# Gram chain of a four-layer convolution kernel: outer products from diagonals and one constant product, copies merged, one link fewer

## The chip, the cores and the metric

The kernel runs on one core of a Trainium2 chip. The metric is device time in microseconds (us), the median of the runs. TensorE is called PE, VectorE DVE, ScalarE ACT, GpSimd POOL; SP is SyncE, which issues most of the DMAs.

## The reference

The input x is 16 images of 64 channels by 128 by 128 pixels, float32. Each of four layers adds to x something computed from a group norm of x (32 groups, so two channels in each).

```python
def _L0_conv_ref(x, conv_w):
    N = H * W
    xf = x.reshape(B, C, N)
    gram = jnp.einsum('bcn,bdn->bcd', xf, xf) / N
    y = jnp.einsum('bcd,bdn->bcn', gram, xf)
    y = y.reshape(B, C, H, W)
    out = jnp.einsum('oc,bchw->bohw', conv_w, y)
    return out
...
x = x + _L0_conv_ref(_gn(x), L0_conv_conv_w)
x = x + _L1_conv_ref(_gn(x))                         # |gx| + |gy| of a 3x3 edge filter in each channel
x = x + _L2_conv_ref(_gn(x), L2_conv_W, L2_conv_b)   # shift of half of the channels by a column, 3x3 conv
x = x + _L3_conv_ref(_gn(x), L3_conv_w_bin, ...)     # 3x3 conv, 1x1 conv, norm over the batch, leaky, clip
```

Layer 0 is linear in the pixels once the Gram matrix of the image (64 by 64) is known. With the channel means mu and the group means and variances, the layer is one 64 by 64 matrix A for each image, and so are the group statistics of its output.

## The kernel before

**Layout.** An image's 64 channels stand twice on the 128 partitions, upper and lower half of the picture, and it is worked in NS = 8 pieces of R = 8 rows of each half. Most matrix products are of 64 columns of weights, and are issued to the two column halves of PE by turns (`small_product` does that for the small ones: two products of 128x64 weights).

**Order of the work.** The order on each engine is written out by hand and kept. A main loop runs over steps; a step is one piece of each of three stages that work on different images at the same time, Layer3, Layer2 and Front (layers 0 and 1: `mix` multiplies by A into the tile `po`, ACT writes the normalized tile `xh`, DVE makes the edge filter from it in `u` and `e`). Each step has quarters 0 to 3. In each quarter the stages issue their share: in quarter 1 the four DVE operations of the edge filter, ahead of quarter 2 the two Abs of ACT on `u` and `e`, in quarter 2 and 3 the DVE operations that read these.

**Gram matrices.** For each image the class Gram reads x with pixels on the partitions (`xr`), ACT copies it to `xw`, and 128 products add up the Gram matrix and the sums in `pg`. Then `gram_chain` is appended to a list of generators, `chains`. At the end of each quarter `tick()` advances each chain to its next `yield`, so every link of a chain is issued behind that quarter's other work. Most links are one PE product or the DVE operations between two products. A link is a quarter of a step after the one before it. The lines `if b > 1: yield` split links for images 2 to 15; image 1 has the shorter chain of nine ticks, and image 0's chain runs by itself, before the loop, in `first_gram`, where ACT copies pieces of image 1's `xr` between links 2 to 6. Images 1 to 6 are prepared at double pace.

**The chain itself.** `gs`: copy of `pg`. `gd`: sum of both halves. `g`: Gram matrix and means `mu`. `st0`: means and the Gram matrix's diagonal. A product with `gavg` takes the average over each group. `rstd` makes 1/sqrt(variance + eps) from that: `me`, `nv`, `var`, Sqrt on ACT into `sd`, then a reciprocal and a refinement to `r`. `vv` holds five columns of means. Four small vectors turned to rows by `pr` and copied to `rw` give an outer product of two rows each, `pc`, so that `cs` is the covariance of the centred channels, twice side by side. `pq` multiplies by the layer's weights `rc`; `ad`, `wbd` and `abd` are A in the shapes needed; `pd`, `pp`, `av` and `pk` give mean and second moment of the layer's output, from which a second `rstd` makes the coefficients `co1` for Front. `coefficients` is the like chain for the norms ahead of layers 2 and 3.

All tiles of the small products lie in one bank of PSUM, and are called `bank` in the profile. All instructions issued through the ordered engines have the line of the helper, L73; they are told apart by the names of their tiles.

Of the kernel before, what the change touches and what calls it, by code (L numbers as in the profile page):

```python
# [10 lines left out]
F32 = mybir.dt.float32  # L11
AF = mybir.ActivationFunctionType
ALU = mybir.AluOpType
AX = mybir.AxisListType

B, C, H, W = 16, 64, 128, 128
P = 128
# [5 lines left out]
EARLY = 3  # L23
CP = 4
GN_EPS = 1e-5
# [19 lines left out]
def single(table, n):  # L45

    for o in range(2):
        planes = [i for m, i, half, _ in table if (m, half) == (n, o)]
        if len(planes) == 1:
# [1 line left out]

NAMES = [("I", P), ("same", P), ("hsame", P), ("gavg", P), ("gmean", P), ("bnavg", P), ("Id", C), ("q", 1),
         ("keep0", 1), ("keep1", 1), ("left", 1), ("right", 1), ("I3", 3 * P), ("lower", 1), ("upper", 1)]
AT = {}
K_END = 0
# [20 lines left out]
def constants():  # L78
    k = np.zeros((P, K_END), np.float32)
    p = np.arange(P)  # L80
    ch = p % C

    def put(name, a):
        k[:, AT[name][0]:AT[name][1]] = a

    same = ch[:, None] == ch[None, :]
    pair = ch[:, None] // 2 == ch[None, :] // 2
    put("I", np.eye(P))
    put("same", same)
    put("hsame", 0.5 * same)  # L90
    put("gavg", 0.25 * pair)
    put("gmean", pair / (2.0 * HW))
    put("bnavg", (ch[:, None] == (p // 2)[None, :]) / (B * HW))
    put("Id", ch[:, None] == np.arange(C)[None, :])
    put("q", 0.25)
    put("keep0", (~((ch >= C // 4) & (ch < C // 2)))[:, None])
    put("keep1", (~(ch < C // 4))[:, None])

    left, right = ch < C // 4, (ch >= C // 4) & (ch < C // 2)
    put("left", left[:, None])  # L100
    put("right", right[:, None])
    put("I3", np.concatenate([np.eye(P) * m[:, None] for m in (left, ~left & ~right, right)], axis=1))
    put("lower", (p < C)[:, None])
    put("upper", (p >= C)[:, None])
    return k
# [3 lines left out]
def tile_kernel(ctx: ExitStack, tc: tile.TileContext, x, cw_h, w2_t, b2, wbin_t, w1_t, b1, gamma, beta, consts, out):  # L109
# [10 lines left out]
    def k(name):  # L120
        return kc[:, AT[name][0]:AT[name][1]]
# [41 lines left out]
    def sv(name, n=1):  # L163
        return small.tile([P, n], F32, tag=name, name=name)
# [16 lines left out]
    def sm(n, rows=P):  # L181
        if n > 8:
            return bank[0:rows, P:P + n]
        turn[0] = (turn[0] + 1) % 16
        return bank[0:rows, 8 * turn[0]:8 * turn[0] + n]
# [72 lines left out]
            if next(c, chains) is chains:  # L258
                chains.remove(c)

    def rstd(mE, eps):

        me = sv("me", 2)
        dve.tensor_copy(me, mE)
        nv = sv("nv")
        dve.scalar_tensor_tensor(nv, me[:, 0:1], me[:, 0:1], me[:, 1:2], op0=ALU.mult, op1=ALU.subtract)
        var = sv("var")
        dve.tensor_scalar(var, nv, -1.0, eps, op0=ALU.mult, op1=ALU.add)
        sd = sv("sd")
        act.activation(sd, var, AF.Sqrt)  # L270
        yield
        r0 = sv("r0")
        dve.reciprocal(r0, sd)

        e = sv("e")
        dve.scalar_tensor_tensor(e, var, r0, r0, op0=ALU.mult, op1=ALU.mult)
        dve.tensor_scalar(e, e, -0.5, 1.5, op0=ALU.mult, op1=ALU.add)
        r = sv("r")
        dve.tensor_mul(r, r0, e)
        return r, me[:, 0:1]  # L280

    def coefficients(st, put, back=None):

        s2 = sv("s2", 2)
        dve.tensor_reduce(s2, st, axis=AX.X, op=ALU.add)
        yield
        pm = sm(2)
        small_product(pm, k("gmean"), s2)
        yield
        r, mean = yield from rstd(pm, GN_EPS)  # L290
        co = sv("co", 2) if back is None else sv("co2", 6)
        dve.tensor_copy(co[:, 0:1], r)
        dve.scalar_tensor_tensor(co[:, 1:2], mean, -1.0, r, op0=ALU.mult, op1=ALU.mult)
        if back is not None:

            dve.reciprocal(co[:, 2:3], r)
            dve.tensor_mul(co[:, 3:4], co[:, 2:3], k("left"))
            dve.tensor_mul(co[:, 4:5], co[:, 2:3], k("right"))
            dve.tensor_add(co[:, 5:6], mean, back)
        put(co)  # L300
# [4 lines left out]
    def gram_chain(b, pg):  # L305

        gs = stp.tile([P, C + 1], F32, tag="gs", name=f"gs_{b}", bufs=1)
        dve.tensor_copy(gs, pg)
        if b > 1:
            yield  # L310
        gd = sm(C + 1)
        small_product(gd, k("same"), gs)
        yield
        g = stp.tile([P, C + 1], F32, tag="g", name=f"g_{b}", bufs=1)
        dve.tensor_scalar_mul(g, gd, 1.0 / HW)
        mu = g[:, C:C + 1]
        st = sv("st0", 2)
        dve.tensor_copy(st[:, 0:1], mu)
        junk0 = stp.tile([P, C], F32, tag="junk0", name=f"junk0_{b}", bufs=1)
        dve.scalar_tensor_tensor(  # L320
            junk0, g[:, 0:C], 1.0, k("Id"), op0=ALU.mult, op1=ALU.mult, accum_out=st[:, 1:2]
        )
        if b > 1:
            yield
        pm = sm(2)
        small_product(pm, k("gavg"), st)
        yield
        r, mean = yield from rstd(pm, GN_EPS)

        vv = sv("vv", 5)  # L330
        dve.tensor_scalar_mul(vv[:, 0:1], mu, -1.0)
        dve.tensor_sub(vv[:, 1:2], mu, mean)
        dve.tensor_copy(vv[:, 2:3], mu)
        dve.tensor_sub(vv[:, 3:4], mu, mean)
        dve.tensor_scalar_mul(vv[:, 4:5], mean, -1.0)
        if b > 1:
            yield
        pr = sm(2 * P, rows=2)
        pe.matmul(pr[:, 0:P], vv[:, 0:2], k("hsame"), start=True, stop=True)
        pe.matmul(pr[:, P:2 * P], vv[:, 2:4], k("hsame"), start=True, stop=True)  # L340
        yield
        rw = stp.tile([2, 2 * P], F32, tag="rw", name=f"rw_{b}", bufs=1)
        dve.tensor_copy(rw, pr)
        if b > 1:
            yield
        pc = sm(C)
        pe.matmul(pc, rw[:, 0:P], rw[:, P:P + C], start=True, stop=True)
        yield

        cs = stp.tile([P, 2, C], F32, tag="cs", name=f"cs_{b}", bufs=1)  # L350
        for s in range(2):
            dve.tensor_add(cs[:, s, :], pc, g[:, 0:C])
        rc = stp.tile([P, C], F32, tag="rc", name=f"rc_{b}", bufs=1)
        dve.tensor_scalar(rc, cwh, r, 0.5, op0=ALU.mult, op1=ALU.mult)
        csf = cs.rearrange("p s c -> p (s c)")
        if b > 1:
            yield
        pq = sm(C)
        small_product(pq, csf, rc)
        yield  # L360
        r2 = sv("r2")
        dve.tensor_mul(r2, r, r)
        for s in range(2):
            rows = slice(s * C, (s + 1) * C)
            dve.tensor_scalar_mul(wbd[rows, rows], pq[rows], r2[rows])
        ad = stp.tile([P, C], F32, tag="ad", name=f"ad_{b}", bufs=1)
        dve.scalar_tensor_tensor(ad, pq, r2, k("Id"), op0=ALU.mult, op1=ALU.add)
        abd = stp.tile([P, P], F32, tag="abd", name=f"abd_{b}", bufs=EARLY + 3)
        dve.tensor_add(abd, wbd, k("I"))
        if b > 1:  # L370
            yield
        pd = sm(C + 3)
        small_product(pd[:, 0:C], csf, ad)
        small_product(pd[:, C:C + 2], abd, vv[:, 2:4])
        small_product(pd[:, C + 2:C + 3], wbd, vv[:, 4:5])
        yield
        pp = stp.tile([P, 2, C], F32, tag="pp", name=f"pp_{b}", bufs=1)
        for s in range(2):
            dve.tensor_mul(pp[:, s, :], pd[:, 0:C], ad)
        av = sv("av", 3)  # L380
        dve.tensor_copy(av, pd[:, C:C + 3])
        if b > 1:
            yield
        pk = sm(1)
        small_product(pk, pp.rearrange("p s c -> p (s c)"), k("q"))
        if b > 1:
            yield
        bias = sv("bias")
        dve.tensor_copy(bias, av[:, 2:3])
        st1 = sv("st1", 2)  # L390
        dve.tensor_add(st1[:, 0:1], av[:, 0:1], bias)
        t = sv("t1")
        dve.scalar_tensor_tensor(t, av[:, 1:2], av[:, 1:2], pk, op0=ALU.mult, op1=ALU.subtract)
        dve.scalar_tensor_tensor(
            st1[:, 1:2], st1[:, 0:1], st1[:, 0:1], t, op0=ALU.mult, op1=ALU.subtract
        )
        if b > 1:
            yield
        pm = sm(2)
        small_product(pm, k("gavg"), st1)  # L400
        yield
        r, mean = yield from rstd(pm, GN_EPS)

        co = stp.tile([P, 4], F32, tag="co1", name=f"co1_{b}", bufs=EARLY + 3)
        dve.tensor_copy(co[:, 0:1], r)
        dve.tensor_sub(co[:, 1:2], bias, mean)
        dve.tensor_mul(co[:, 1:2], co[:, 1:2], r)
        dve.reciprocal(co[:, 2:3], r)
        dve.tensor_copy(co[:, 3:4], mean)
        lead[b] = abd, co  # L410

    def gram_product(pg, w):
# [696 lines left out]
```

## Time and profile before

| | |
|---|---|
| median of 3 runs | 2795.21 us (2790.94 to 2795.56) |
| profiled execution | 2793.34 us, span of the instructions 2791.6 us |
| granted PE clock, mean | 0.900 |
| PE busy | 2232.5 us (80%), 14836 matmuls |
| DVE busy | 2200.6 us (79%), 3751 instructions |
| ACT busy | 2115.3 us (76%), 3177 instructions |
| POOL busy | 865.2 us (31%), 1350 instructions |
| DMA | 685.97 MB, mean 246 GB/s |

Busy time is the union of an engine's intervals. A float32 matmul appears as two records. In a line of the profile the tile written stands left of the arrow, those read right of it; `bank<-kc,vv` is a product that writes the small bank from a constant and `vv`. A line of waits says which engine and tile waited for whom, total us, times, longest us. A timeline line has start and duration in us, and in brackets how long the engine had been idle and what ended it. The duration of neighbouring DVE operations overlaps, so that the start-to-start distance says what an operation costs.

The span has four stages: the start to 47 us with image 0's Gram matrix and chain bare; 47 to 350 us, in which Layer2 and Layer3 come in and the Gram matrices of images 1 to 6 are made; 350 to 2325 us with all stages; and an end of 470 us in which layer 3's norm over the batch is applied and everything is read and written once more.

### The profile page before, as it was taken

Reading aid. Unit: us, or ns where it says so; the run is one execution under the profiler, and the core shown is the slowest. Engines: PE = TensorE matmul, PEld = TensorE weight load, DVE = VectorE, ACT = ScalarE, POOL = GpSimd, SP = SyncE. Lnnn points to the kernel's source line nnn. Section 1 sums busy time; section 2 is a strip of 40 time slices with the busy share of each in tenths; the row PEclk is TensorE's granted clock in tenths of the full one; section 3 lists DMA queues with packets and bytes.
Section 4 is the critical chain, followed back from the end, with each engine's and each line's share of the span. In section 5 each row is a group of like instructions: output and inputs, shape, how many; then the busy total and the mean of one; then the engine's idle time right before and its main releaser. Section 6 shows DMA issues by size and latency. Waiting matters only on the chain. (4 is left out here: it accounts for less than half of the span.)

```text
span 2791.6 us, 46444 instructions
## 1 busy us (share of the span) xinstructions
PE 2232.5 (80%) x14836; PEld 1097.1 (39%) x14836; DVE 2200.6 (79%) x3751; ACT 2115.3 (76%) x3177; POOL 865.2 (31%) x1350
## 2 busy tenths in 40 slices
PE   6578899999999999999999999999999995000000
PEld 4234444534454444353534343466666641000000
DVE  4998999898989898989898989999996435333332
ACT  4666789888888888888888888998997667333332
POOL 2054434342434343334343434444444310000000
PEclk8689999999999999999999999999999997555555
DMA  7789878888888888888888867888887768999999
GB/s 193 196 224 235 223 203 237 218 228 211 222 222 219 222 221 224 221 220 220 223 219 225 215 182 198 213 205 216 208 208 185 214 194 277 419 420 420 420 420 390
DMA packets 680290, 685.97 MB, mean 246 GB/s; under 512 B 60096, under 2 KB 580448, under 8 KB 680048
## 3 DMA queue, kind: packets, MB, share of 16 engines
q1 hardware_dynamic: 654896, 613.83, 74.4%
q0 software_dynamic: 25152, 69.18, 10.1%
q8 instruction: 120, 1.97, 0.3%
q14 instruction: 122, 1.00, 0.1%
HBM read 346.23 MB, written 268.44 MB: 220 GB/s over the span
## 5 line engine op out<-in xcount | busy, mean ns | idle before, releaser
L73 PE MATMUL two<-d,w 128*64 128x508 f32 (+2 forms) x2560 | 898.7, 587 | 0.0
L73 PE MATMUL two<-d,wi 128*64 128x508 f32 (+3 forms) x1536 | 629.8, 576 | 0.0
L73 POOL DMA_DIRECT2D qd<-d x512 | 270.8, 531 | 892.5 <-issue 330.2
L73 PE MATMUL two<-qd,pk 128*64 128x512 f32 (+1 forms) x1024 | 518.6, 588 | 3.1 <-DMA qd<-d 2.4
L73 POOL TENSOR_SCALAR edges<-v,co 64x8 f32<-64x8 f32 x512 | 330.0, 645 | 355.6 <-ACT v L73 240.4
L73 PE MATMUL po<-x,abd 128*64 128x512 f32 x1024 | 385.9, 626 | 50.3 <-ACT xh L73 47.7
L73 PEld LDWEIGHTS two<-d,w 128*64 128x64 f32 x2560 | 297.4, 136 | 289.5 <-issue 219.5
L73 PE MATMUL one<-v,w 128*64 128x508 f32 (+2 forms) x1600 | 409.6, 578 | 0.0
L73 PE MATMUL one<-v,wi 128*64 128x508 f32 (+3 forms) x1536 | 408.9, 590 | 0.0
L73 DVE TENSOR_TENSOR d<-v 128x512 f32<-128x512 f32 (+1 forms) x512 | 346.0, 679 | 41.5 <-POOL v L73 16.7
L73 ACT COPY qd<-d 64x512 f32<-64x512 f32 x512 | 315.4, 616 | 21.0 <-DVE d L73 14.6
L73 ACT ACTIVATE xh<-po,co 128x128 f32<-128x128 f32 (+1 forms) x480 | 274.9, 621 | 62.4 <-PE po L73 58.9
L73 DVE SCALAR_TENSOR_TENSOR e<-e 128x1032 f32<-128x1032 f32 (+1 forms) x256 | 313.4, 1224 | 0.0
L73 DVE SCALAR_TENSOR_TENSOR y<-two,c 128x1024 f32<-128x1024 f32 x128 | 156.1, 1220 | 129.8 <-ACT v L73 71.5
L73 PEld LDWEIGHTS two<-d,wi 128*64 128x64 f32 x1536 | 196.3, 135 | 146.4 <-issue 110.7
L73 POOL TENSOR_SCALAR v<-v,kc 128x9 f32<-128x9 f32 x256 | 234.8, 930 | 11.9
L73 ACT ACTIVATE v<-x,co 128x512 f32<-128x512 f32 (+2 forms) x368 | 234.9, 705 | 0.0
L73 PEld LDWEIGHTS one<-v,w 128*64 128x64 f32 x1600 | 163.4, 137 | 178.3 <-issue 128.6
L73 PEld LDWEIGHTS one<-v,wi 128*64 128x64 f32 x1536 | 156.2, 138 | 163.0 <-issue 126.1
L73 ACT ACTIVATE u<-u 128x1024 f32<-128x1024 f32 x128 | 135.3, 1057 | 88.4 <-DVE u L73 87.0
L73 DVE SCALAR_TENSOR_TENSOR u<-xh 128x1170 f32<-128x1170 f32 x128 | 175.7, 1373 | 6.0 <-ACT xh L73 4.4
L73 PEld LDWEIGHTS two<-qd,pk 128*64 128x64 f32 x1024 | 128.6, 136 | 120.3 <-issue 81.2
(165 smaller groups left out, 3463.7 us busy)
## 6 DMA issues: line engine op xcount, KB each, us to landing
x<-in_x SPq DMA_DIRECT2D x256, 256.0 KB, 4.2
x_d<-u SPq DMA_DIRECT2D x512, 128.0 KB, 3.7
y_d<-y SPq DMA_DIRECT2D x512, 128.0 KB, 4.2
x_d<-x SPq DMA_DIRECT2D x496, 128.0 KB, 2.6
xr<-in_x SPq DMA_DIRECT2D x120, 512.0 KB, 6.0
qd<-d POOLq DMA_DIRECT2D x256, 130.0 KB, 3.0
qd<-d POOLq DMA_DIRECT2D x256, 129.8 KB, 3.6
v<-x_d SPq DMA_DIRECT2D x448, 72.1 KB, 3.0
```

The source lines that it names most:

```text
L73: return self.tc.keep_in_program_order(call(*args, **kwargs))
```

## The change

The outer products are made in another way. Two diagonal matrices `dd` (the constant `Id` times a column of `vv`) are multiplied by a constant matrix of 0.5 (`all`), which gives each vector as rows on all partitions; the multiplication by the other vector and the subtraction from `g` are done on DVE in `t0` and `cs`. With that the product `pc` and the copy `rw` are gone, and so is their link (two `yield`s for images 2 to 15). `rstd` writes to tiles that it is given, takes eps as an option (the first one in a Gram chain has it added to the diagonal), and gives Sqrt the factor -1 in place of a DVE operation. Copies into `co`, `co1` and `bias` are gone, and the two operations of `pp` are one.

```diff
-    def rstd(mE, eps):
+    def rstd(mE, r, me, eps=None):
-        me = sv("me", 2)
         dve.tensor_copy(me, mE)
         nv = sv("nv")
         dve.scalar_tensor_tensor(nv, me[:, 0:1], me[:, 0:1], me[:, 1:2], op0=ALU.mult, op1=ALU.subtract)
-        var = sv("var")
-        dve.tensor_scalar(var, nv, -1.0, eps, op0=ALU.mult, op1=ALU.add)
+        if eps is not None:
+            dve.tensor_scalar_sub(nv, nv, eps)
         sd = sv("sd")
-        act.activation(sd, var, AF.Sqrt)
+        act.activation(sd, nv, AF.Sqrt, scale=-1.0)
         yield
...
     def coefficients(st, put, back=None):
...
-        r, mean = yield from rstd(pm, GN_EPS)
         co = sv("co", 2) if back is None else sv("co2", 6)
-        dve.tensor_copy(co[:, 0:1], r)
+        me = sv("me", 2)
+        r, mean = co[:, 0:1], me[:, 0:1]
+        yield from rstd(pm, r, me, GN_EPS)
...
     def gram_chain(b, pg):
...
-            junk0, g[:, 0:C], 1.0, k("Id"), op0=ALU.mult, op1=ALU.mult, accum_out=st[:, 1:2]
+            junk0, g[:, 0:C], GN_EPS, k("Id"), op0=ALU.add, op1=ALU.mult, accum_out=st[:, 1:2]
...
-        r, mean = yield from rstd(pm, GN_EPS)
-        vv = sv("vv", 5)
-        dve.tensor_scalar_mul(vv[:, 0:1], mu, -1.0)
-        dve.tensor_sub(vv[:, 1:2], mu, mean)
-        dve.tensor_copy(vv[:, 2:3], mu)
-        dve.tensor_sub(vv[:, 3:4], mu, mean)
-        dve.tensor_scalar_mul(vv[:, 4:5], mean, -1.0)
+        r, me = sv("r"), sv("me", 2)
+        yield from rstd(pm, r, me)
+        vv = sv("vv", 3)
+        dve.tensor_copy(vv[:, 0:1], mu)
+        dve.tensor_sub(vv[:, 1:2], mu, me[:, 0:1])
+        dve.tensor_scalar_mul(vv[:, 2:3], me[:, 0:1], -1.0)
+        dd = stp.tile([P, 2, C], F32, tag="dd", name=f"dd_{b}", bufs=1)
+        for s in range(2):
+            dve.tensor_scalar_mul(dd[:, s, :], k("Id"), vv[:, s:s + 1])
         if b > 1:
             yield
-        pr = sm(2 * P, rows=2)
-        pe.matmul(pr[:, 0:P], vv[:, 0:2], k("hsame"), start=True, stop=True)
-        pe.matmul(pr[:, P:2 * P], vv[:, 2:4], k("hsame"), start=True, stop=True)
+        pr = sm(2 * C)
+        small_product(pr, k("all"), dd.rearrange("p s c -> p (s c)"))
         yield
-        rw = stp.tile([2, 2 * P], F32, tag="rw", name=f"rw_{b}", bufs=1)
-        dve.tensor_copy(rw, pr)
-        if b > 1:
-            yield
-        pc = sm(C)
-        pe.matmul(pc, rw[:, 0:P], rw[:, P:P + C], start=True, stop=True)
-        yield
+        t0 = stp.tile([P, C], F32, tag="t0", name=f"t0_{b}", bufs=1)
+        dve.scalar_tensor_tensor(t0, pr[:, 0:C], vv[:, 0:1], g[:, 0:C], op0=ALU.mult, op1=ALU.subtract)
         cs = stp.tile([P, 2, C], F32, tag="cs", name=f"cs_{b}", bufs=1)
         for s in range(2):
-            dve.tensor_add(cs[:, s, :], pc, g[:, 0:C])
+            dve.scalar_tensor_tensor(cs[:, s, :], pr[:, C:2 * C], vv[:, 1:2], t0, op0=ALU.mult, op1=ALU.subtract)
...
-        for s in range(2):
-            dve.tensor_mul(pp[:, s, :], pd[:, 0:C], ad)
+        dve.tensor_mul(
+            pp, pd[:, 0:C].unsqueeze(1).to_broadcast([P, 2, C]), ad.unsqueeze(1).to_broadcast([P, 2, C])
+        )
...
-        bias = sv("bias")
-        dve.tensor_copy(bias, av[:, 2:3])
+        bias = av[:, 2:3]
...
-        r, mean = yield from rstd(pm, GN_EPS)
-        co = stp.tile([P, 4], F32, tag="co1", name=f"co1_{b}", bufs=EARLY + 3)
-        dve.tensor_copy(co[:, 0:1], r)
-        dve.tensor_sub(co[:, 1:2], bias, mean)
-        dve.tensor_mul(co[:, 1:2], co[:, 1:2], r)
+        co = stp.tile([P, 5], F32, tag="co1", name=f"co1_{b}", bufs=EARLY + 3)
+        r, mean = co[:, 0:1], co[:, 3:4]
+        yield from rstd(pm, r, co[:, 3:5], GN_EPS)
+        dve.scalar_tensor_tensor(co[:, 1:2], bias, mean, r, op0=ALU.subtract, op1=ALU.mult)
         dve.reciprocal(co[:, 2:3], r)
-        dve.tensor_copy(co[:, 3:4], mean)
```

The two products that use `vv` further down now take its columns 0 to 1 and 2 in place of 2 to 3 and 4.

More of the change, by code (lines that the diff above doesn't have):

```diff
@@ L50, in single @@
             return o, planes[0]
-NAMES = [("I", P), ("same", P), ("hsame", P), ("gavg", P), ("gmean", P), ("bnavg", P), ("Id", C), ("q", 1),
+NAMES = [("I", P), ("same", P), ("all", P), ("gavg", P), ("gmean", P), ("bnavg", P), ("Id", C), ("q", 1),
          ("keep0", 1), ("keep1", 1), ("left", 1), ("right", 1), ("I3", 3 * P), ("lower", 1), ("upper", 1)]
@@ L89, in constants @@
     put("same", same)
-    put("hsame", 0.5 * same)
+    put("all", np.full((P, P), 0.5))
     put("gavg", 0.25 * pair)
@@ L275, in rstd @@
         e = sv("e")
-        dve.scalar_tensor_tensor(e, var, r0, r0, op0=ALU.mult, op1=ALU.mult)
-        dve.tensor_scalar(e, e, -0.5, 1.5, op0=ALU.mult, op1=ALU.add)
-        r = sv("r")
+        dve.scalar_tensor_tensor(e, nv, r0, r0, op0=ALU.mult, op1=ALU.mult)
+        dve.tensor_scalar(e, e, 0.5, 1.5, op0=ALU.mult, op1=ALU.add)
         dve.tensor_mul(r, r0, e)
-        return r, me[:, 0:1]
     def coefficients(st, put, back=None):
@@ L373, in gram_chain @@
         small_product(pd[:, 0:C], csf, ad)
-        small_product(pd[:, C:C + 2], abd, vv[:, 2:4])
-        small_product(pd[:, C + 2:C + 3], wbd, vv[:, 4:5])
+        small_product(pd[:, C:C + 2], abd, vv[:, 0:2])
+        small_product(pd[:, C + 2:C + 3], wbd, vv[:, 2:3])
         yield
         pp = stp.tile([P, 2, C], F32, tag="pp", name=f"pp_{b}", bufs=1)
-        for s in range(2):
-            dve.tensor_mul(pp[:, s, :], pd[:, 0:C], ad)
+        dve.tensor_mul(
+            pp, pd[:, 0:C].unsqueeze(1).to_broadcast([P, 2, C]), ad.unsqueeze(1).to_broadcast([P, 2, C])
+        )
         av = sv("av", 3)
```

## The prediction

> **What bounds the kernel now.** I read the page's slices first, then busy time by window, then waits engine by engine, then the timeline.
>
> ```profile
> PE   6578899999999999999999999999999995000000
> DVE  4998999898989898989898989999996435333332
> ACT  4666789888888888888888888998997667333332
> ```
>
> A slice is 69.8 us. From slice 5 to 33 (about 350 to 2325 us) PE shows 9 everywhere, so TensorE looks like the bound. Before that VectorE (DVE) carries the 9s; after 2340 us the chain of waits is DMA alone, and this change touches nothing there. The Gram chains run between 30.9 and 1715 us. The Trainium skill ("Perfetto Trace Analysis", Identifying the Most-Contended Engine) warns that matmul busy time is a bad measure because matmuls are pipelined, so I asked who waits for whom in one image's period (136.8 us; the chain of image 10 starts at 953.2 and ends at 1030.8). Busy time by window, columns us, PE, PEld, DVE, ACT, POOL:
>
> ```profile
> 953.20:1038.70 85.50, 84.47 (x464) 37.82 (x459) 82.98 (x166) 77.69 (x122) 34.13 (x52) 1.00 0.85 226
> 1038.70:1090.00 51.30, 51.30 (x464) 24.14 (x466) 44.03 (x62) 44.38 (x69) 16.35 (x31) 1.00 0.84 214
> ```
>
> The waits of DVE alone: the first line is its only wait over the gap limit in 953 to 1038.7, the next two are the largest of 1038.7 to 1090.
>
> ```profile
> DVE d L73 <- POOL v L73: 0.5, 1, 0.5
> ...
> DVE y L73 <- ACT junk L73: 3.4, 1, 3.4
> DVE two L73 <- PE two L73: 2.0, 1, 2.0
> ```
>
> And the timeline where the stretches meet:
>
> ```profile
> 1034.39 1.06 ACT L73 ACTIVATE u<-u 128x1024 f32<-128x1024 f32 x1 [2.03 <-DVE u L73]
> 1038.69 1.08 PE L73 MATMUL po<-x,abd 128*64 128x512 f32 x4 [1.03 <-ACT xh L73]
> ```
>
> So a period has two halves. While a chain runs, DVE never waits for PE; it goes without a break except 0.52 us for POOL, and at 1038.69 PE itself has caught up and waits for ACT, which waited for DVE. (1.03 us is PE's idle time by modelled ends; start to start it loses 1.6 us.) After that PE leads and DVE waits for it. The chain lies wholly in DVE's half. PE's 9s hide this, because both are above 97%.
>
> **What the skill says of the operations.** "TensorEngine Tiling (Array Packing)", Key Properties: changing the tiling mode drains TensorE. Agrees: the old outer product uses 128*2 and 2*128 tiles among 128*64 ones. I price an insertion as the time from the eighth matmul before to the eighth after, less their streaming (0.427 us for a pair of 512-column halves). `bank<-kc,vv` then costs 1.122 to 1.126 us in all ten chains of the PE-heavy stage, though its columns need 0.43; `bank<-rw` costs 0.53. An ordinary 64-column `small_product` costs 0.14. "VectorE: DVE Perf Modes", Rules for kernel authors, says to minimize the op count, since a flush follows each op anyway. Agrees in part: a dependent 1-column op costs 0.19 us start to start, an independent one 0.07.
>
> **Part by part, DVE, for one image.** Start-to-start costs from the chain of image 10; minus is a saving.
> - `var` gone in the first rstd: nv 0.285 and var 0.071 become one nv with an independent follower, 0.14 (as `junk`): -0.215. In the three others `tensor_scalar_sub` replaces it, 0.
> - `vv` 5 to 3, `dd` added: five at 0.065 before; after, 0.2 until `dd` may read vv, then 0.13 and 0.16 for two 128x64 ops (as `rc`, 0.16): +0.165.
> - `rw` copy gone:
>
> ```profile
> 983.80 0.41 DVE L73 COPY rw<-bank 2x256 f32<-2x256 f32 x1
> 984.14 0.15 DVE L73 TENSOR_REDUCE s<-st 128x2 f32<-128x16 f32 x1
> ```
>
> -0.335.
> - `t0` added (a PSUM op with a dependent follower: `ad` lasts 0.284): +0.32. The two `cs` become scalar_tensor_tensor, 0.13 to 0.20 each (as `ad`, 0.202): +0.14.
> - `pp` in one op of 128 columns: -0.07. The trace has no such broadcast from PSUM; bounds: 0 to -0.1.
> - `bias` copy gone: -0.18. `co1` loses two copies and a subtraction, 0.65 to 0.345: -0.305. `coefficients` writes r in place, twice: -0.14.
> Sum: -0.62 us. New forms are bounded at +-0.3.
>
> Beside this the schedule moves. For images 2 to 15 two links go (the `rw` one and the product that followed), so all from t0/cs on runs two quarter-steps, 8.6 us, earlier, and the group t0, cs, cs, rc, 0.88 us, lands at 984, ahead of the POOL wait at 989.55. There the added +0.43 fills most of the 0.52 that DVE spent idle. Net at that point -0.07, after it -0.42 (cs gone from there), -0.07, -0.07, -0.18, -0.305: **about -1.1 us a period**.
>
> **PE.** 1.124 + 0.53 go; the product of `dd` comes. 128 columns in normal halves: 0.14 + 0.107 for 64 more columns a pass = 0.25. PE saves 1.40 us per image, but in DVE's half: I count nothing, as PE waits 1.6 us for ACT at its end already, and would wait longer. If that cover is gone, 1.4 is what it is worth.
>
> **The wait that moves.** For images 7 to 15 the second rstd's Sqrt goes from the end of quarter 3 to the end of quarter 1 (for 2 to 6 from 0 to 2, behind the Abs, where the first one stands already). ACT must then wait for all four sobel ops, me, nv and the subtraction before it may start the two Abs:
>
> ```profile
> 1017.04 1.06 ACT L73 ACTIVATE u<-u 128x1024 f32<-128x1024 f32 x1 [0.92 <-DVE u L73]
> ```
>
> "TensorE: Matmul & The Clock Gate" (Architectural detail) says ACT's queue is strictly first in, first out; the trace agrees, every ACT start is in program order. Abs u would start at 1018.06 (end of `e`) - 0.63 saved so far + 0.19 + 0.25 + 0.19 + 0.22 (Sqrt) = 1018.3, 1.26 later. Queued behind: the other Abs, xh, c, the layer-3 twins; PE waits for xh and has 3.0 us to give (1.6 + 1.4). DVE's next reader of Abs u is at 1020.6 - 0.8 = 1019.8, Abs ends 1019.4: covered by 0.4. ACT's 2.03 us at 1034.39 covers the rest; less the Sqrt that left 1025 (0.2), it leaves ACT at -1.0 instead of -1.1. So I take **-1.0 for each of images 6 to 15, -10 us**. DMAs: none is added, removed or moved past a queue.
>
> **Image 0** runs bare at the start:
>
> ```profile
> 34.98 0.41 DVE L73 COPY rw<-bank 2x256 f32<-2x256 f32 x1 [0.50 <-PE bank L73]
> 36.07 0.36 DVE L73 TENSOR_TENSOR cs<-bank,g 128x64 f32<-128x64 f32 x2 [0.68 <-PE bank L73]
> 36.34 0.25 DVE L73 TENSOR_SCALAR rc<-cwh,r 128x64 f32<-128x64 f32 x1
> ```
>
> var -0.2; from r at 34.00 to rc at 36.34: vv and dd until PE starts 0.48, PE 0.67 (as `pe<-xe,abd`, same 128 columns), t0 0.3, cs 0.4 = 1.85 against 2.34, -0.5; pp -0.07; co -0.25. **-1.0**. The copies to `xw` are on other links now, but their DMAs land one per 1.57 us and the last ends at 40.05, before the Sqrt.
>
> **Images 1 to 5** (70 to 350 us): DVE is 86 to 96% busy and waits rarely; -0.62 each is -3.1. Some of it sinks into waits there (1.3 us on POOL at 192 and 251, 5.7 us at 267.54 on ACT held by an xr load), so I take -2.
>
> Sum -10 - 1 - 2 = **-13 us** against the profiled execution's own 2793.34 (span 2791.6): 2780.3. The median shown, 2795.21, is 1.9 higher, so I forecast 2782. About 0.2%, 5.6 us, is what a measurement of this kernel can tell from no change.
>
> **Rivals.**
> - PE is the bound after all: 1.4 x 10 = 14, plus image 0 to 5 in full, 4.1, and a little: -19, 2776. For it: slices of 9. Against: PE waits for ACT once a period, DVE does not wait for PE in the chain's half. 12%.
> - Absorbed: the POOL wait moves with ACT and `dd`, `t0` and `cs` are dearer than taken (+0.3), so a period keeps 0.2 to 0.3, early savings vanish: -4, 2791. For it: ACT and POOL were late at 989.5 for reasons other than the chain. Within 0.2%. 20%.
> - Slower: the Sqrt in quarter 1. It is ACT's 1.26 us against 2.03 us of slack at 1034.39 and 0.4 at the Abs reader. If Abs is over 0.4 us later than I have it, DVE's own gx op waits, and each further 0.1 goes on the path; once ACT and not DVE sets the end of this half, what DVE saves is no help and an image loses the whole 1.26. In images 7 to 15 that is +11.3, less 1 for image 0 and 1 for the others: +9, 2804. For it: ACT waits for DVE at this very place already. 23%.
> - The forecast: 42%; its own range -7 to -18. What is left, 3%, goes with the PE case's side. That it does not do what it says (DVE count unchanged) I exclude: each removed line is one instruction in the trace.
>
> Faster 0.57, same 0.20, slower 0.23. The range 2773 to 2801 takes in the PE case, the absorbed one and half of the slower one.
>
> **What would show it.** DVE has 3751 instructions; per image 6 fewer in the chain and 2 in the coefficients: 3623. `rw` and 128*2 tiles gone, PE 32 records fewer. In a period: PE's wait before po at the end grows from 1.6 to about 2 or more us, the POOL wait at `d` near 0, an ACT wait of over 2 us ahead of `sd`, period 135.8 instead of 136.8. A period shortened by 1.4 with no PE wait would mean the PE case; DVE waiting for `u` or ACT ahead of gx, the slower one. The forecast is wrong if the period does not shrink, or if the stage before 350 us moves by more than 5 us.

## The result, and the profile after

The changed kernel takes 2782.32 us (median of 5 runs, 2780.48 to 2783.86) against 2795.21 us before: ratio 0.9958, 95% interval 0.9947 to 0.9969, 12.9 us faster; in time the interval is 8.7 to 14.8 us. The profiled execution has a span of 2779.2 us, 12.4 less. The forecast was 2782. In three later series the kernel before had medians of 2793.3 to 2794.0 us, from 18 to 44 runs each; against those the changed kernel's 2782.32 is some 11 to 12 us less.

The page's busy tenths after, in 40 slices of the span:

```profile
PE   6478899999999999999999999999999995000000
DVE  5999999898989898989898989999996435333332
ACT  4766889898989898989898988999997667333332
```

The picture of the engines is the same. DVE has 3623 instructions, as counted, and PE 32 matmul records fewer. The same two windows of image 10's period (the columns are us, PE, PEld, DVE, ACT, POOL, with instructions behind each):

```profile
943.40:1028.90 85.50, 84.34 (x462) 38.25 (x460) 83.58 (x159) 78.36 (x123) 30.85 (x52) 1.00 0.84 227
1028.90:1079.70 50.80, 50.80 (x464) 24.03 (x462) 42.95 (x60) 43.66 (x68) 16.07 (x31) 1.00 0.84 214
```

And the four largest waits of DVE in the whole period after:

```profile
DVE y L73 <- ACT junk L73: 3.4, 1, 3.4
DVE two L73 <- PE two L73: 2.0, 1, 2.0
DVE y L73 <- ACT u L73: 1.2, 1, 1.2
DVE d L73 <- POOL v L73: 0.4, 2, 0.2
```

The wait of 0.5 for POOL inside the chain's half is gone; what is left for POOL comes later, 0.2 at a time. The wait that moved is in the timeline of ACT, and PE's wait after it:

```profile
1008.82 0.20 ACT L73 ACTIVATE sd<-nv 128x1 f32<-128x1 f32 x1 [1.77 <-DVE nv L73]
1008.93 1.04 ACT L73 ACTIVATE u<-u 128x1024 f32<-128x1024 f32 x1
...
1011.86 1.11 ACT L73 ACTIVATE xh<-po,co 128x512 f32<-128x512 f32 x2
...
1013.02 1.08 PE L73 MATMUL po<-x,abd 128*64 128x512 f32 x4 [1.16 <-ACT xh L73]
```

ACT stands 1.77 us for the Sqrt before it may do the Abs; the xh behind it comes later, and PE waits for that xh. Before, PE's big wait for ACT stood at 1038.69, the end of the half. Now it stands one step earlier in the order of the work, at 1013, and from there to the period's end the profile shows no wait of PE: PE sets the pace for the rest of the period.

To see where the time goes I use two measures from the traces. **Period**: the median of the eight distances between the `gs` copies of images 7 to 15: 136.80 us before, 136.32 after. **Lead**: how much earlier the edge filter's first operation (`u<-xh` on DVE) of a given image starts than in the kernel before:

| at us of the kernel before | 47.5 | 193 | 394 | 461 | 935 | 1619 | 2065 | end |
|---|---|---|---|---|---|---|---|---|
| lead of the changed kernel, us | 1.9 | 3.8 | 6.6 | 7.6 | 9.7 | 12.0 | 12.6 | 12.4 |

So in this trace some 7.6 us are won by 461 us, and only about 0.5 a period after that. How far such a number can be trusted is said below, with the kernel that has its links back from image 7.

### The profile page after: what moved, and what is told of

Read it like the earlier page. It is cut to its first block, busy times and chain, and to the rows that moved or that the text cites. A ratio compares the mean times of both kernels' runs of the same rounds, so it can differ in the third digit from the quotient of the medians.

```text
span 2779.2 us, 46241 instructions
## 1 busy us (share of the span) xinstructions
PE 2220.0 (80%) x14804; PEld 1125.6 (41%) x14804; DVE 2193.7 (79%) x3623; ACT 2113.9 (76%) x3177; POOL 837.1 (30%) x1350
## 5 line engine op out<-in xcount | busy, mean ns | idle before, releaser
L73 PE MATMUL two<-d,w 128*64 128x508 f32 (+2 forms) x2560 | 884.4, 586 | 0.0
L73 PE MATMUL two<-d,wi 128*64 128x508 f32 (+3 forms) x1536 | 616.6, 577 | 0.0
L73 POOL TENSOR_SCALAR edges<-v,co 64x8 f32<-64x8 f32 x512 | 308.4, 602 | 370.4 <-ACT v L73 276.3
L73 PE MATMUL one<-v,wi 128*64 128x508 f32 (+3 forms) x1536 | 396.6, 596 | 2.5 <-issue 2.5
L73 PE MATMUL one<-v,w 128*64 128x508 f32 (+2 forms) x1600 | 398.1, 578 | 0.5 <-ACT c L73 0.5
L73 PE MATMUL po<-x,abd 128*64 128x512 f32 x1024 | 351.9, 617 | 51.9 <-ACT xh L73 48.9
L73 POOL TENSOR_SCALAR v<-v,kc 128x9 f32<-128x9 f32 x256 | 228.2, 905 | 11.9
```

What stands on the lines that cost most here:

```text
L73: return self.tc.keep_in_program_order(call(*args, **kwargs))
```

## Experiments

Theory A is the prediction's: while a chain runs DVE sets the pace, PE's saving is worth nothing there, and the Sqrt in quarter 1 takes a part of the gain back. Theory B is that PE is the bound and its 1.4 us an image were what was won.

**Links back, for images 2 to 15.**

```diff
         small_product(pr, k("all"), dd.rearrange("p s c -> p (s c)"))
         yield
+        if b > 1:
+            yield
+            yield
```

> The changed kernel with two empty links put in behind the product of dd for images 2 to 15, so that t0, cs and all that follows stand in the same quarters as before the change, the second Sqrt at the end of quarter 3 again. Theory A (DVE sets the pace while a chain runs; the early Sqrt holds ACT, ACT holds po, and PE loses there the lead that the cheaper product gave it): images 7 to 15 keep about 1.0 us each in place of the 0.5 seen, so some 5 us under the changed kernel, 2777 (2774 to 2780), and PE's wait before po is at the end of the chain's half again, 2 us or more. Theory B (PE is the bound and its 1.4 us are what was won): PE's work is the same, so 2782 within 2. Theory C (that the later links come two quarters earlier is itself what helps): slower than the changed kernel by 4 or more, 2786.

Measured: 2780.54 us (ratio to before 0.9956, 0.9943 to 0.997), not told apart from the changed kernel by the runs; the span is 2776.1. The total lies just outside Theory A's range and would suit Theory B too, so it decides nothing between them. The period does: 135.78, 1.02 less than before and 0.54 less than the changed kernel's. ACT's timeline at the same place:

```profile
1007.24 1.06 ACT L73 ACTIVATE u<-u 128x1024 f32<-128x1024 f32 x1 [0.83 <-DVE u L73]
1008.38 1.06 ACT L73 ACTIVATE e<-e 128x1024 f32<-128x1024 f32 x1
```

No Sqrt, and the Abs waits for `u` alone, as before the change (0.92 there). Theory A's 1.0 an image is what came, and Theory C is out, since nothing became slower. PE's wait ahead of po at the end of the half is back too, but not at the 2 us expected: it is 0.42 us in this period and at most 0.9 in others, and ahead of it stands 0.24 us (at most 1.2) on the DMA for `qd`. The early lead was smaller here (5.5 at 394), which is why the span shrank by less than nine periods of 0.54.

**Only the second rstd back.** The two empty links stand right ahead of the last product with `gavg`.

> The changed kernel with the two empty links right ahead of the last product with gavg for images 2 to 15: cs, rc, wbd, ad, abd, pp and st1 stay two quarters earlier, the second rstd alone goes back to quarter 3. Theory A with the Sqrt as the only cause: like the kernel with the two links behind dd, 2777 (2774 to 2780). If it is rather abd and wbd ahead of the third layer's rstd that cost (ACT waits 1.9 us for nv there), then it stays at 2781 to 2783. Theory B: 2782 within 2.

Measured: 2782.13 us (0.9959, 0.9946 to 0.9971), period 136.03. Half of the loss: of the 0.54 that the earlier links cost an image, the second Sqrt has 0.29 and the other links 0.25. The trace points to where the 0.25 comes from: as in the changed kernel, ACT's Abs one step before lies 0.7 us behind its place in the period, and wbd, ad and abd now stand ahead of the third layer's `nv`, for which ACT waits. The expectation named these as alternatives, and by the periods both are true, though each share is not much above the 0.17 by which the period differs between two traces of the same code (see the parts by image).

**Merged operations alone**, with the old outer product and five columns of `vv` (in this kernel `all` holds the constant that the kernel before used there):

```diff
-        dd = stp.tile([P, 2, C], F32, tag="dd", name=f"dd_{b}", bufs=1)
...
-        small_product(pr, k("all"), dd.rearrange("p s c -> p (s c)"))
+        pe.matmul(pr[:, 0:P], vv[:, 0:2], k("all"), start=True, stop=True)
+        pe.matmul(pr[:, P:2 * P], vv[:, 2:4], k("all"), start=True, stop=True)
...
+        dve.tensor_copy(rw, pr)
...
+        pe.matmul(pc, rw[:, 0:P], rw[:, P:P + C], start=True, stop=True)
```

> The changed kernel with the old outer product (five vv, pr, rw, pc, two links more): only the merged and removed DVE operations are left, 0.9 us of DVE an image (var 0.215, bias 0.18, co1 0.305, coefficients 0.14, pp 0.07), all PE work and all quarters as before. Theory A: 0.9 for images 6 to 15, some 3 us for 1 to 5, 0.5 for image 0: 12 under the kernel before, 2783 (2780 to 2787). Theory B: PE has nothing less to do, 2793 to 2795.

Measured: 2785.7 us against 2793.26 before (0.997, 0.9959 to 0.9982), period 136.08. PE has nothing less to do and a period still falls by 0.72; Theory B allowed nothing. The early gain was missing: a lead of 0.6 at 461 us, where some 3.5 were expected.

**The outer product alone**, all other operations as before:

> The kernel before with the new outer product alone (three vv, dd, one product, t0, new cs, two links fewer): PE has 1.4 us an image less to do, DVE 0.29 more, the second Sqrt stands in quarter 1. Theory A: DVE's 0.29 lie partly in its idle time ahead of d, the Sqrt costs up to 0.5 an image, image 0 wins 0.5: no gain, 2793 to 2799. Theory B: 1.4 for each of images 6 to 15, 2781 (2779 to 2784).

Measured: 2793.39 us against 2793.26 (0.9999, 0.9991 to 1.0008), period 136.97. PE's 1.4 us less an image bought nothing in the long stage. This alone does not rule out Theory B, because the early links, which cost 0.54 an image in the changed kernel, are in this kernel too; the next experiment leaves them out. The lead of 2.7 at 461 us was gone in part by the end (1.7).

**PE's cost put back**, on the kernel with links back from image 7:

```diff
         small_product(pr, k("all"), dd.rearrange("p s c -> p (s c)"))
+        if b > 2 * EARLY:
+            for _ in range(2):
+                pe.matmul(bank[0:2, 2 * P:3 * P], vv[:, 0:2], k("all"), start=True, stop=True)
+            pe.matmul(bank[:, 2 * P:2 * P + C], kc[0:2, 0:P], kc[0:2, 0:C], start=True, stop=True)
```

> The kernel with links back from image 7, and for these images three more products behind that of dd, whose result nobody reads: two with 128*2 tiles and 128 columns and one with 2*128 and 64 columns, so that PE has about the 1.65 us an image to do that pr and pc cost, and DVE nothing more. Theory A (PE has slack while a chain runs): its waits for ACT and for DMA there shrink and an image costs at most 0.3 more, under 3 in all: 2780 to 2783. Theory B (PE is the bound): 1.65 for nine images, 2795.

The timeline of PE shows the added products at work:

```profile
971.96 0.60 PE L73 MATMUL bank<-kc,vv 128*2 128x128 f32 x4
972.49 0.43 PE L73 MATMUL bank<-kc 2*128 2x64 f32 x2
972.85 0.64 PE L73 MATMUL two<-d,w 128*64 128x512 f32 x1
```

Measured: 2779.19 us (0.9948, 0.9935 to 0.9962), period 135.77. The stream of products behind them stands about 1.5 us later in the period than without them, and the period is the same to 0.04. At the end of the half PE's wait for ACT has shrunk: without the added products PE stood idle 0.60 us ahead of po,

```profile
1029.70 1.08 PE L73 MATMUL po<-x,abd 128*64 128x512 f32 x4 [0.60 <-ACT xh L73]
```

with them the line has no idle time over the profile's limit:

```profile
1030.25 1.08 PE L73 MATMUL po<-x,abd 128*64 128x512 f32 x4
```

PE had slack, and the products sank into it. Theory B is out.

**DVE cost added**, on the same kernel:

```diff
+        if b > 2 * EARLY:
+            for _ in range(4):
+                dve.tensor_scalar_mul(junk0, k("Id"), vv[:, 0:1])
```

> The kernel with links back from image 7, and for these images four more DVE operations of 128x64 behind that product (each 0.16 us start to start, result unread): 0.65 us an image of DVE's time and no PE work. Theory A (DVE sets the pace while a chain runs): 0.5 to 0.65 for each of nine images, +5, 2785 to 2786. Theory B: nothing, 2780.

```profile
983.79 1.11 DVE L73 TENSOR_SCALAR junk<-kc,vv 128x64 f32<-128x64 f32 x4
984.82 0.28 DVE L73 SCALAR_TENSOR_TENSOR t<-bank,vv,g 128x64 f32<-128x64 f32 x1
```

The four took 1.03 us from the first start to the next operation, not 0.65: all write the same elements, and none starts before the one ahead of it has ended. Measured: 2788.84 us against 2793.57 before (0.9982, 0.9974 to 0.9989), and against 2780.11 of the kernel without them; period 137.00, 1.19 more than the 135.81 without. In image 10's period every later `u<-xh` up to the end of the half starts 1.05 us later than without them, so nothing absorbs the added time. DVE's time goes to the end one for one and a little over, PE's not at all. One place in the chain was tried for each of the two.

**Parts by image.** Three kernels have the changed chain for some images alone, and the old one, with the old `coefficients`, for the rest.

> The kernel before with the changed chain for image 0 alone (old chain and old coefficients for all others; a further constant of 128 columns is loaded). If the bare chain is worth what the changed kernel shows at the first edge filter, this starts it 1.0 to 1.9 us earlier. If DVE sets the pace from there to 350 us, 1 us or more is left at 390 us and at the end: 2792. If DMA or other waits in 70 to 350 us take it up, nothing is left: 2793 to 2795.

> The kernel before with the changed chain for images 1 to 6 alone. By DVE's sums 0.48 each (coefficients are the old ones), 3 us by 460 us; the changed kernel shows 5.7 between 47 and 460 us. If the quarter in which the links stand matters more than the sums, it is 4 to 6 here too: 2788 to 2790. If the early gain needs image 0's as well, 2 or less.

> The kernel before with the changed chain for images 7 to 15 alone, old coefficients. Until 470 us the kernel before to 0.3 us; then 0.4 an image (0.5 less a part of 0.14), some 4 us: 2789 to 2791. If PE were the bound, 1.4 an image, 2781.

Measured, against 2793.97 before: image 0 2794.32 (1.0, 0.9992 to 1.0008), images 1 to 6 2789.26 (0.9983, 0.9975 to 0.999), images 7 to 15 2790.28 (0.9989, 0.9983 to 0.9996). Image 0's chain does bring its filter forward (0.9 us at 47.5); the lead is 0.8 at 193 us, -0.9 at 252, 0.5 at 394, 0.6 at 935 and 0.2 at the end. The runs of this kernel are good to 2.2 us either way and cannot tell a gain of 1 us from none. Images 1 to 6 give 5.0 us of lead by 461 us, 4.4 of it at the end, which is the alternative in which the quarter of the links matters more than the sums. Images 7 to 15 give 0.37 each.

In the stage of images 7 to 15 the first two of these kernels run the same code as the kernel before. Their periods are 136.84 and 136.97, against its 136.80: differences of 0.2 between periods mean nothing.

**Links back from image 7 alone** keeps the changed kernel's early schedule:

> The changed kernel with the two empty links behind the product of dd for images 7 to 15 alone. Up to 400 us it should be the changed kernel (6.6 us ahead of the kernel before at the ninth image's quarter of the loop, image 3), from there on gain 1.0 us an image like the kernel with links back for all, in place of 0.5: 4 to 5 us under the changed kernel, 2778 (2776 to 2780). If the early lead of the changed kernel is chance of the schedule, or the links of image 7 and later do not carry, it stays at 2781 to 2783.

Measured: 2780.11 us (0.9948, 0.9935 to 0.996), period 135.81. It and the kernel with all links back are the fastest by trace, 1.0 less a period than before, but the runs do not separate them from the changed kernel. The expected total, 2776 to 2780, was just missed, and so was the early part: the lead at 394 us is 3.7, not 6.6. The lead at 47.5 us was 0.4 here and 1.9 in the changed kernel's trace, though both run the same code up to there. Five traces of this document have the same code up to 541 us (the changed kernel, this one, those with PE's and DVE's cost added, and the one with one link back): their leads are 0.2 to 1.9 us at 47.5 and 4.2 to 7.6 at 461, and the changed kernel's trace has the largest of both. So 3 us of an early lead can be chance of one execution, and totals of single traces are not compared closer than that.

**One link back** in place of two:

> The changed kernel with one empty link, not two, behind the product of dd for images 7 to 15: the second Sqrt stands at the end of quarter 2, behind the two Abs, and wbd and abd no longer ahead of the third layer's rstd. Theory A: an image gains 0.9 to 1.1 as with two links, 2780. If it must be quarter 3, the gain an image is that of the changed kernel, 0.5, or less: 2782 to 2785.

A miss: 2790.27 us (0.9986, 0.998 to 0.9993), period 137.10, more than before the change. The second Sqrt is out of the Abs's way as intended, and other links collide:

```profile
983.06 0.28 PE L73 MATMUL bank<-s,kc 128*64 128x2 f32 x4 [0.54 <-DVE cs L73]
...
986.96 0.16 DVE L73 COPY me<-bank 128x2 f32<-128x2 f32 x1 [1.39 <-PE bank L73]
...
987.60 0.20 ACT L73 ACTIVATE sd<-nv 128x1 f32<-128x1 f32 x1 [2.27 <-DVE nv L73]
...
994.79 0.49 ACT L73 ACTIVATE v<-x,edge_lower 128x128 f32<-128x128 f32 x1 [2.96 <-DVE edge_lower L73]
```

t0 and cs now stand in the quarter in which the third layer's chain multiplies by `gmean`; by the profile that product waits for cs. DVE then stands 1.39 us for a product in the small bank. It is not that one, which was done at 983.34: the product that ends just before DVE goes on is the chain's own, `bank<-rc,cs`:

```profile
986.64 0.28 PE L73 MATMUL bank<-rc,cs 128*64 128x64 f32 x2
```

Later wbd and abd stand ahead of `edge_lower`, contrary to the expectation, and ACT waits 2.96 us for that in place of 1.8.

## Why the prediction was right or wrong

**The bound: right** while a chain runs. PE's cost put back costs nothing, DVE's cost added goes to the end in full, and the merged operations gain without PE. The outer product alone, which is all of PE's saving, gains nothing, but has the early links against it. (The chain of waits turns to DMA alone at 2357 us and not at 2340; nothing rests on it.)

**DVE's sum: right in its terms.** In the trace after, t0 costs 0.316 us start to start (0.32 forecast), the cs 0.20 and 0.19, dd 0.159 and 0.162, pp 0.201. At 86 us of image 10's period (counted from its `gs`) DVE stands 1.11 us earlier than before, and 1.1 was the forecast.

The wait for POOL went, as said, but there is more to it than operations that fill it. What DVE waited for was a POOL operation on 9 columns. Before the change, in the changed kernel, and with the two links back:

```profile
985.32 4.20 POOL L73 TENSOR_SCALAR v<-v,kc 128x9 f32<-128x9 f32 x2
...
975.53 0.62 POOL L73 TENSOR_SCALAR v<-v,kc 128x9 f32<-128x9 f32 x2
...
976.09 2.35 POOL L73 TENSOR_SCALAR v<-v,kc 128x9 f32<-128x9 f32 x2
```

In each of images 7 to 15 the first of the two takes 3.9 us before the change, 0.33 after and 0.61 with the links back. It starts at the same place of the period, 32.1 us after `gs`, but DVE's operations beside it have moved. With the links back, t0, cs and rc stand behind this wait as cs and rc did before the change, so they do not fill it, and it is gone all the same; with the merged operations alone POOL again takes 3.9 us and DVE waits 0.53. That fits the periods: the kernel with the links back gains 1.02, the merged operations alone 0.72, although by the prediction's sum they leave DVE 0.29 us less to do. Why so small an operation takes 0.33 or 3.9 us was not tested.

**Images 6 to 15: too large, -10 forecast.** From the `gs` of image 6 to that of image 15 the changed kernel's lead grows from 5.8 to 12.0 us, that is 6.2. The failed step is the cover of the moved Sqrt. It was put at 1.26 us later for the Abs, and "ACT's 2.03 us at 1034.39 covers the rest". The Abs came 1.66 us later in the period, and ACT's slack did cover it for DVE; but the step let PE off with "3.0 us to give", and PE had no such lead there. Against its place in the period before, PE is 0.9 to 1.0 us early at the po and qd products from 979 to 984, 0.2 late at the po at 996 and 1.45 late at the po at 1013. Once late it cannot catch up, because it is full from there to the period's end; all it gains is that the wait which stood at 1038.69 is gone, and it ends the period 0.47 early. DVE's lead of 1.11 shrinks to that 0.47 in PE's half. The slack at the end of the half was no slack at its middle. The Sqrt was not alone either: the links that moved with it, wbd and abd by the trace, cost 0.25 of the 0.54. So the slower rival's mechanism, ACT held by a Sqrt two quarters early, is at work, at half the saving and not more; it went by way of PE's wait for xh and not, as that rival had it, by DVE's gx.

**Images 1 to 5: too small, -2 forecast** (with image 6, -3). The chain of images 1 to 6 alone gives 4.4 to 5.0, more than its DVE sum of 0.48 each. That waits would eat a part was wrong: from the first filter to 461 us DVE's waits for ACT's `u`, POOL's `v` and PE's `pg` fell from 15.6 to 10.9 us in that trace, and its other waits grew by some 2. Why they fell is open.

**Image 0: right for the chain, open for the end, -1.0 forecast.** From `gs` to the first `u<-xh` takes 16.4 to 16.6 us in four traces with the old outer product and 15.1 to 15.9 in eight with the whole new chain. In the kernel with the new chain for image 0 alone 0.5 to 1.0 us of it is left in most of the long stage and 0.2 at the end, less than the runs can tell. (40.05 us is the end of ACT's last copy to `xw`, not of a DMA; nothing rests on that either.)

**The total was right because these errors offset each other**, too little early against too much late, and that is luck: in the other traces of the same code the early part is 2 to 3 us smaller. In the long stage the parts add up by their periods: -0.72 for the merged operations and +0.17 for the outer product, -0.48 for both. In the totals they give -7.6 and +0.1 us, and the three groups of images about -8 together, against -12.9. The groups lack the copies of `coefficients`, an estimated 2.2 us from 0.14 an image; the rest lies in the stage before 461 us, is within the intervals of the runs taken together, and its cause is open.

**The rivals.** The PE case is refuted. Absorbed: the outer product alone has its result, but not its cause, since the wait for POOL is gone there too and t0 and cs cost what was taken. Of the signs that the prediction named, the counts of DVE and PE and the wait for POOL came. The wait ahead of po did not grow, it moved forward to 1013; ACT's wait ahead of `sd` is 1.77 us and not over 2; the period is 136.32 and not 135.8. One sign of being wrong came as well: the stage before 350 us was not to move by more than 5 us, and the changed kernel's lead at 339 us is 6.1. In the four other traces of the same code it is 2.7 to 3.9.

## What to carry to other kernels

Where two engines are both over 97% busy, ask in each stretch who waits for whom, and settle it by adding a known cost to one engine at a time: 1.5 us of PE cost nothing here and 1.0 us of DVE cost 1.2. In an order written by hand, taking a link out of a chain moves every later link to another place among the other work, and that is to be priced link by link: here one position gave 1.0 us an image, another 0.5 and a third a loss. When a wait goes away, look too at how long the operation that ended it took: here POOL's had become shorter. Slack read at the end of a stretch cannot be spent in its middle by an engine that is full from there on.

## What the runs showed of the hardware that was not expected

Four 128x64 DVE operations that write the same elements started 0.28 to 0.29 us apart, where the two of `dd`, which write different halves of one tile, started 0.16 apart.

A POOL operation of 128x9 took 0.33, 0.61 or 3.9 us, the same in nine of nine images of a kernel. The kernels differ in which DVE operations ran beside it; whether that is the cause was not tested.
